# A four-layer graph network on one core: the attention stage of layer 0 with the variance per node by Newton steps, two tiles of layer 1 made early, and loads seven chunks ahead

## The chip, the core and the metric

The kernel runs on one core of a Trainium2 chip. The metric is the device time of one launch in microseconds. Before the change it is the median of three runs, 1951.25 us (1949.47 to 1952.59).

The names in a profile: PE is TensorE (matrix products, into PSUM), PEld its loading of weights, DVE is VectorE, ACT is ScalarE, POOL is GpSimd, SP is SyncE, which here only issues transfers. SPq and POOLq are the queues of transfers that these two issue.

## What is computed

`x` has 8 batches of 2048 nodes with 64 features. There are four layers; each takes `h = max(layernorm(x), 0)` and adds its result to `x`. The change touches the end of layer 0 and the start of layer 1:

```python
# layer 0, end: two candidates per node, mixed by attention scores
def attn_scores(f):
    return jnp.tanh(f @ fcW + fcb) @ av
pair = jnp.stack([industry, g], axis=2)
coefs2 = jax.nn.softmax(attn_scores(pair), axis=-1)
out = jnp.einsum('bnk,bnkf->bnf', coefs2, pair)
x = x + out
# layer 1
h = jnp.maximum(_layernorm(x, axis=-1), 0.0)       # (x - m) / sqrt(v + eps)
h = jnp.matmul(h, W)
s_src, s_dst = jnp.matmul(h, a_src), jnp.matmul(h, a_dst)
e = leaky_relu(s_src[:, :, None] + s_dst[:, None, :], 0.2)
attention = softmax(jnp.where(adj > 0.5, e, NEG_INF), axis=2)
x = x + elu(jnp.matmul(attention, h))
```

A softmax over two candidates is a sigmoid of the difference of their scores, and a sigmoid is a tanh of half the argument. So layer 0's end is: the tanh of each candidate's projection, their difference, the product with `av`, a tanh, and `out = g + (1 + tanh) * (industry - g) / 2`.

## The kernel before

**Layout.** Two batches with 64 features each fill the 128 partitions; this is a pair, and there are four (`p` = 0 to 3). The 2048 nodes lie along the free dimension, in four chunks of 512 (`c`). So the stage at the end of layer 0 works on 16 chunks `(p, c)`, numbered from 0 in the order of pairs. For layer 1 the nodes are also cut into 16 tiles of 128 (`m`).

**The attention stage of layer 0** (the loop at the end of `layer0`, lines 1452 to 1536). `gT[p]`, which the trace calls `hn`, holds `g` of a pair; `industry` lies in DRAM as `ind_dram`. Each chunk goes through these functions:

- `first` loads `iv` from `ind_dram` (line 1475, on SP's queue) and makes `th_s`, the tanh of `fcW` times `iv`: two matmuls into `pf` (PSUM, two buffers for all), one activation of 128x1024 on ScalarE. In the trace a float32 matmul shows as two passes.
- `second` does the same for `g` and then overwrites `iv` with `iv - g/2` on VectorE.
- `differ` subtracts the two tanh tiles (VectorE, 128x1024).
- `third` multiplies by `av` into `pd` (two buffers) and takes the tanh in place.
- `fourth` makes `(tanh + 1) * iv`. For pair 0 it adds `g` and the old `x` (`xo`, loaded by SP, line 1513) on VectorE and SP stores the sum to `x1_dram` (line 1504). For the other pairs POOL issues a transfer that adds the tile to `x1_dram` (line 1500), which the trace calls `xd`; `g` itself is added to it by three transfers of 1 MB from POOL (line 1534, `xd<-hn`).
- After the last chunk of a pair, `late_tile` has POOL load one of the last four tiles of the adjacency, `aTl`, into the memory of that pair's `hn` (line 2188).

The loop runs the functions interleaved: iteration `i` does `first` and `second` of chunk `i + 1`, `third` of `i - 1`, `differ` of `i` and `fourth` of `i - 2`.

**Layer 1's start for pair 0** is woven into this loop. `first_neighbours` is a generator; from iteration 5 the loop takes two of its steps per iteration. For two chunks at a time it makes the mean (a matmul with `avg`, 1/64 in two blocks), subtracts it (`xc`), squares (`q`, ScalarE), makes the variance by a second matmul with `avg` (`var`, which repeats it on all 64 rows of a batch), takes ln and exp on ScalarE for the inverse root, and scales and clips `xc`. Then `ph` is the product with `W1x`: per tile of 128 nodes the 128 features and four scores. `vd`, `wd` and `rs` are exponentials of the scores, and `hS` is the features times `vd`. Last come `R`, a copy of `rs` along the free dimension on every partition (16 matmuls into `pb`, four copies), and `pr`, its transpose, which goes to DRAM for the second half of the nodes. `ph`, `mean`, `var` and `pb` share the two PSUM tags "ln" and "h".

**Layer 1's attention** (`attend`): for each tile `m`, VectorE makes two tiles `pt` of 128x1024, `max(R, wd) * adjacency` (line 1733, one for each batch of the pair; this stands for the leaky relu, the mask and the exponential at once), and TensorE multiplies them with `hS` into `o` and with `vd` into `dn`. Between the tiles, the next pair's norm and maps are woven in by `neighbour_steps`, which reads `x` back from `x1_dram` (line 1575).

**What sets the order.** Instructions go to each engine's own queue and are carried out in that queue's order; a waiting one holds all behind it. A scheduler may reorder what is written, except what goes through `InOrder` (line 631 in the trace: it records the instruction and keeps it in program order) or through `kit.mm` while `kit.strict` is set (line 734). In this stage TensorE, ScalarE (`A`) and VectorE (`V`) are in written order; SP's and POOL's transfers are not. Tile pools hand out memory that may have belonged to an earlier stage, and then the first write waits for the last use there.

## Time and profile before

| what | value |
|---|---|
| median of three runs | 1951.25 us |
| profiled execution: its time, its span | 1953.49 us, 1951.7 us |
| TensorE busy, mean granted clock | 1888.2 us (97%), 0.989 |
| VectorE busy | 1191.2 us (61%) |
| ScalarE busy | 437.4 us (22%) |
| first score matmul of the stage | 374.57 us |
| first `o` matmul of layer 1 | 462.13 us |

How to read it: times are microseconds from the start of the span. A row of the stretches gives, for a stretch of time, its length, then the busy time and the number of instructions of each engine, then the granted TensorE clock as a share of full speed, the busy share of the 16 DMA engines and their rate. A row of the waits gives who waited for whom: the sum, the number of times, the longest. A row in order of time gives start, duration, engine, line, operation, output and inputs, shapes, and in brackets how long the engine was idle before it and what ended that. A wait for several things is put down to the one that came last.

### The profile page before, as it was taken

How to read it: one execution, taken by the hardware profiler on the slowest of the kernel's cores; microseconds unless marked ns; L12 is line 12 of the kernel's file. 1: busy time of each engine (PE TensorE's matmuls, PEld its weight loads, DVE VectorE, ACT ScalarE, POOL GpSimd, SP SyncE). 2: the span in 40 equal slices, each digit the busy share in tenths (PEclk: the TensorE clock that was granted, in tenths of full speed). 3: DMA queues.
4: the chain of work that ended last, by engine and by line, in shares of the span. 5: the costliest groups of instructions: out<-in, count | busy, mean ns of one | idle time of the engine just before them, and what ended most of it. 6: DMA issues, size and time to landing. Idle time of an engine off the chain costs nothing.

```text
span 1951.7 us, 23508 instructions
## 1 busy us (share of the span) xinstructions
PE 1888.2 (97%) x9060; PEld 1141.7 (58%) x9060; DVE 1191.2 (61%) x1917; ACT 437.4 (22%) x923; POOL 310.3 (16%) x435
## 2 busy tenths in 40 slices
PE   7999999888999999999999999999999999999997
PEld 6877767423323232247775567765577755677653
DVE  8676499667899998973327652346723266523465
ACT  6322355564212110111220101301112201012100
POOL 4111187311000000000002110111200022101122
PEclk9999899999999999999999999999999999999999
DMA  7656385374121212214200112101022011121000
GB/s 211 174 177 180 121 249 148 97 200 82 41 62 40 61 43 55 65 23 116 60 22 25 30 43 71 49 10 30 24 74 59 22 25 30 43 71 49 5 19 12
DMA packets 86363, 142.43 MB, mean 73 GB/s; under 512 B 33801, under 2 KB 34057, under 8 KB 83569
## 3 DMA queue, kind: packets, MB, share of 16 engines
q1 hardware_dynamic: 65200, 83.86, 14.8%
q0 software_dynamic: 21040, 56.98, 12.0%
q8 instruction: 73, 1.20, 0.3%
q14 instruction: 50, 0.40, 0.1%
HBM read 106.85 MB, written 37.09 MB: 74 GB/s over the span
## 4 chain that ended last, share of the span: by engine, by line
PE 74%; issue 14%; DVE 4%; DMA 3%; POOL 3%; ACT 1%; SPq 0%; POOLq 0%; DVEq 0%; ACTq 0%
PE acc L734 33%; PE u L734 13%; PE o L734 6%; PE dn L734 3%; PE py L734 3%; PE pgs L734 2%; PE acc L1058 2%; PE pd L734 2%; PE var L734 1%; PE mean L734 1%; DMA iv<-ind_dram 1%; DMA at<-in_adjT 1%; DVE pt L1733 1%; PE pv L734 1%; PE pm L734 1%
## 5 line engine op out<-in xcount | busy, mean ns | idle before, releaser
L734 PE MATMUL acc<-aT,parts 128*128 128x512 f32 x1664 | 462.0, 421 | 0.0
L734 PEld LDWEIGHTS acc<-aT,parts 128*128 128x128 f32 x1664 | 306.6, 188 | 111.8 <-issue 51.3
L734 PE MATMUL u<-W3f,y 64*128 64x512 f32 x1024 | 243.2, 589 | 0.0
L1733 DVE SCALAR_TENSOR_TENSOR pt<-R,wd,aT 128x1024 f32<-128x1024 f32 x192 | 236.1, 1279 | 9.7 <-DMA R<-r_dram 4.7
L734 PE MATMUL o<-pt,hS 128*64 128x512 f32 x1024 | 237.2, 599 | 0.8 <-DVE pt L1733 0.6
L2136 DVE TENSOR_TENSOR pr<-u,embf 128x512 f32<-128x512 f32 x256 | 170.7, 688 | 110.2 <-PE u L734 103.2
L734 PEld LDWEIGHTS u<-W3f,y 64*128 64x128 f32 x1024 | 102.3, 187 | 118.0 <-issue 118.0
L734 PEld LDWEIGHTS o<-pt,hS 128*64 128x64 f32 x1024 | 68.4, 136 | 159.9 <-issue 149.2
L734 PE MATMUL u<-W3f,v 64*128 64x512 f32 x512 | 135.0, 596 | 0.0
L2148 POOL TENSOR_TENSOR fold<-fold 128x256 f32<-128x256 f32 x64 | 47.7, 746 | 498.4 <-DVE fold L2147 498.4
L734 PE MATMUL dn<-pt,vd 128*32 128x512 f32 x1024 | 123.1, 598 | 0.0
L1952 DVE TENSOR_TENSOR yb<-py,cb_f 128x512 f32<-128x512 f32 x32 | 22.1, 691 | 161.3 <-PE py L734 161.3
L1058 PE MATMUL acc<-at,Y 128*128 128x512 f32 x384 | 104.7, 415 | 0.0
L734 PE MATMUL acc<-aTl,parts 128*128 128x512 f32 x384 | 98.8, 395 | 0.0
L2140 DVE TENSOR_TENSOR pr<-pr 128x512 f32<-128x512 f32 x128 | 88.2, 689 | 2.2
L2042 POOL TENSOR_TENSOR bq<-bq,xp 128x512 f32<-128x512 f32 x16 | 20.6, 1289 | 430.1 <-ACT xp L2025 430.1
L1733 DVE SCALAR_TENSOR_TENSOR pt<-R,wd,aTl 128x1024 f32<-128x1024 f32 x64 | 79.8, 1282 | 12.4 <-PE dn L734 8.2
L734 PEld LDWEIGHTS u<-W3f,v 64*128 64x128 f32 x512 | 57.3, 186 | 49.6 <-issue 36.1
L734 PEld LDWEIGHTS acc<-aTl,parts 128*128 128x128 f32 x384 | 71.4, 188 | 16.2
L1058 PEld LDWEIGHTS acc<-at,Y 128*128 128x128 f32 x384 | 70.7, 194 | 14.6 <-issue 1.3
L734 PEld LDWEIGHTS dn<-pt,vd 128*32 128x32 f32 x1024 | 26.9, 108 | 80.9 <-issue 75.9
L1966 DVE TENSOR_TENSOR parts<-tp,parts 128x512 fp32r<-128x512 f32 x16 | 11.1, 692 | 85.7 <-ACT parts L1965 85.7
(354 smaller groups left out, 2688.6 us busy)
## 6 DMA issues: line engine op xcount, KB each, us to landing
at<-in_adjT POOLq DMA_DIRECT2D x32, 512.0 KB, 5.5
raw<-in_adjT SPq DMA_DIRECT2D x64, 256.0 KB, 3.4
aT<-in_adjT POOLq DMA_DIRECT2D x12, 1024.0 KB, 6.2
xp<-xd SPq DMA_DIRECT2D x45, 256.0 KB, 3.0
R<-r_dram SPq DMA_DIRECT2D x14, 512.0 KB, 3.8
hlo<-lo_dram POOLq DMA_DIRECT2D x18, 235.1 KB, 3.7
hhi<-hi_dram POOLq DMA_DIRECT2D x18, 235.1 KB, 3.4
hi_dram<-hi SPq DMA_DIRECT2D x16, 264.0 KB, 3.4
```

Source lines behind the costliest of these rows:

```text
L734: one = self.nc.tensor.matmul(*args, **kw)
L1058: mm(acc[p], Y[h][:, m, p, :], at[:, k, :], start=m + h == 0, stop=m == NT - 1 and h == 1)
L1733: nc.vector.scalar_tensor_tensor(pt, R[b2], wd[:, m, b2 : b2 + 1], aT[m][:, s].bitcast(FP), op0=OP.max, op1=OP.mult)
L1952: nc.vector.tensor_tensor(yb, py, bias[:, None, :].to_broadcast([P, 4, P]), op=OP.add)
L1966: nc.vector.tensor_tensor(lo, tp, hi.bitcast(FP), op=OP.subtract)
L2042: nc.gpsimd.tensor_add(bq, bq, xp)
L2136: nc.vector.tensor_tensor(a, u[h], emb[:, i, 8 * w : 8 * w + 8, None].to_broadcast([P, 8, F]), op=OP.mult)
L2140: nc.vector.tensor_add(pr[h], pr[h], a)
L2148: nc.gpsimd.tensor_add(fold[:, :, 0:2, :], fold[:, :, 0:2, :], fold[:, :, 2:4, :])
```

## The change

The variance moves behind the product with `W1x`. The centred `x` is only clipped at zero, not scaled; since the inverse root is positive, the scale commutes with the clip and the product. For each tile of 128 nodes a further small matmul multiplies the squares with two columns of `avg`, which gives the variance per node and batch, with the nodes on the partitions, beside the features and the scores in `ph`. ScalarE copies the features to `hS`, VectorE copies scores and variance to `raw`. When all 16 tiles are there, VectorE makes the inverse root of 128x32 numbers at once: a first guess by integer operations on the bits and three Newton steps. The scores are scaled by it, and `hS` is scaled by its product with `vd`, a quarter in the stage and three quarters in the first tiles of layer 1's attention. So there is no ln in the stage.

The generator gives way to a `plan`: for each engine and each iteration of the loop, which functions are called. The norm begins in iteration 4 and the last of it stands in iteration 17; `R` is made in iterations 14 and 15, and the `pt` tiles of tiles 0 and 1 (`edge`) in 16 and 17. For this the pool of `pt` is opened before the stage; the tanh tiles come from it too.

The loads of `iv` leave `first` and go to `fetch`: seven before the first matmul, four of them in turn with the loads of `xo`, and then one per iteration for the chunk six after the present one. The pool has eight buffers, not nine. SP's and POOL's transfers of the stage now keep the written order (`S`, `G`), the late adjacency tiles among them, and the three 1 MB adds stand in iterations 3, 7 and 11 rather than 1, 4 and 8.

```diff
-        io = s0.enter_context(tc.tile_pool(name="o_io", bufs=9, reuse_waits="tile"))
+        io = s0.enter_context(tc.tile_pool(name="o_io", bufs=8, reuse_waits="tile"))
...
-            th = sb.tile([P, 2, CW], FP, tag="th", name="th_s", bufs=5)
+            th = one.pt.tile([P, HN], FP, tag="pt", name="th_s").rearrange("p (b n) -> p b n", b=2)
             act.activation(th, pf, AF.Tanh, bias=fcb, scale=f)
             return th
 
+        def fetch(i):
+            p, c = chunks[i]
+            ivs[i] = io.tile([P, CW], FP, tag="iv", name="iv")
+            S.dma_start(out=ivs[i], in_=ind_dram[p, :, cols(c)])
+
         def first(i):
-            p, c = chunks[i]
-            iv = ivs[i] = io.tile([P, CW], FP, tag="iv", name="iv")
-            nc.sync.dma_start(out=iv, in_=ind_dram[p, :, cols(c)])
-            ths[i] = scores(iv, 2.0)
+            ths[i] = scores(ivs[i], 2.0)
...
-                nc.gpsimd.dma_start(out=x1_dram[p, :, cols(c)], in_=df, accum_op=OP.add)
+                G.dma_start(out=x1_dram[p, :, cols(c)], in_=df, accum_op=OP.add)
...
+        G = InOrder(tc, nc.gpsimd)
+        for i in range(3):
+            fetch(i)
+        for c in range(NCW):
+            fetch(3 + c)
+            xs.append(sb.tile([P, CW], FP, tag="x", name="xo", bufs=NCW))
+            S.dma_start(out=xs[c], in_=t["xT"][0, :, cols(c)])
         first(0)
         kit.strict = False
         first(1)
-        for c in range(NCW):
-            xs.append(sb.tile([P, CW], FP, tag="x", name="xo", bufs=NCW))
-            nc.sync.dma_start(out=xs[c], in_=t["xT"][0, :, cols(c)])
         second(0)
-        steps = one.first_neighbours(xs, V, A)
+        near = one.first_neighbours(xs, V, A)
 
         for i in range(len(chunks) + 2):
-            if i > 4:
-                next(steps, None)
+            near("DVE", i)
             if 0 < i < len(chunks) - 1:
                 first(i + 1)
             if i < len(chunks) - 1:
                 second(i + 1)
+            near("PE0", i)
             if 0 < i <= len(chunks):
                 third(i - 1)
+            near("PE", i)
             if i < len(chunks):
                 differ(i)
             if i > 1:
                 fourth(i - 2)
-            if i > 4:
-                next(steps, None)
-            if i in (1, 4, 8):
+            if 0 < i and i + 6 < len(chunks):
+                fetch(i + 6)
+            near("V2", i)
+            near("ACT", i)
+            if i in (3, 7, 11):
                 p = 1 + i // 4
-                nc.gpsimd.dma_start(out=x1_dram[p], in_=gT[p], accum_op=OP.add)
-        for _ in steps:
-            pass
+                G.dma_start(out=x1_dram[p], in_=gT[p], accum_op=OP.add)
...
+        self.lasting = ExitStack()
+        self.pt = self.lasting.enter_context(tc.tile_pool(name="att_pt", bufs=6, side="right", reuse_waits="tile"))
...
+        raw = sb.tile([P, NT, 6], FP, name="raw", bufs=1)
...
-                mm(var[k], kit.avg, q[k], start=True, stop=True)
...
-                A.activation(q[k], var[k], AF.Ln, bias=kit.eps)
-            for k in range(2):
-                A.activation(q[k], q[k], AF.Exp, scale=-0.5)
...
-                V.scalar_tensor_tensor(xc[k], xc[k], 0.0, q[k], op0=OP.max, op1=OP.mult)
...
-                    A.activation(vd[:, ms, :], ph[:, :, P : P + 2], AF.Exp, scale=0.2)
-                for ms, ph in two:
-                    V.tensor_copy(sc[:, ms, :], ph[:, :, P:])
-                    V.tensor_tensor(
-                        hS[:, ms, :].rearrange("p t (b f) -> p t b f", b=2),
-                        ph[:, :, 0:P].rearrange("p t (b f) -> p t b f", b=2),
-                        vd[:, ms, :, None].to_broadcast([P, 2, 2, F]), op=OP.mult,
-                    )
...
+        def centre(c):
+            mean[c] = ps.tile([P, CW], FP, tag=("ln", "h")[c % 2], name="mean")
+            mm(mean[c], kit.avg, xs[c], start=True, stop=True)
+
+        def centred(c):
+            xc[c] = sb.tile([P, CW], FP, tag="xc", name="xc")
+            V.tensor_sub(xc[c], xs[c], mean.pop(c))
+
+        def squared(c):
+            q[c] = sb.tile([P, CW], FP, tag=("x", "q")[c % 2], name="q", bufs=1)
+            A.activation(q[c], xc[c], AF.Square)
+
+        def clipped(c):
+            V.tensor_scalar(xc[c], xc[c], 0.0, None, op0=OP.max)
+
+        def maps(c):
+            for g in range(2):
+                ph = ps.tile([P, 2, P + 6], FP, tag=("ln", "h")[g], name="ph")
+                for j in range(2):
+                    n = slice((2 * g + j) * P, (2 * g + j + 1) * P)
+                    mm(ph[:, j, 0 : P + 4], xc[c][:, n], kit.W1x, start=True, stop=True)
+                    mm(ph[:, j, P + 4 :], q[c][:, n], kit.avg[:, 0:P:F], start=True, stop=True)
+                out.append((NC4 * c + 2 * g, ph))
+
+        def mapped():
+            for m, ph in out:
+                A.activation(hS[:, m : m + 2, :], ph[:, :, 0:P], AF.Copy)
+                V.tensor_copy(raw[:, m : m + 2, :], ph[:, :, P:])
+            out.clear()
+
+        def guess():
+            I32 = mybir.dt.int32
+            V.tensor_scalar(var, raw[:, :, 4:6], EPS, None, op0=OP.add)
+            V.tensor_scalar(rstd.bitcast(I32), var.bitcast(I32), 1, None, op0=OP.logical_shift_right)
+            V.tensor_scalar(rstd.bitcast(I32), rstd.bitcast(I32), -1, 0x5F3759DF, op0=OP.mult, op1=OP.add)
+
+        def newton():
+            V.tensor_tensor(nw, rstd, rstd, op=OP.mult)
+            V.scalar_tensor_tensor(nw, nw, -0.5, var, op0=OP.mult, op1=OP.mult)
+            V.scalar_tensor_tensor(rstd, nw, 1.5, rstd, op0=OP.add, op1=OP.mult)
+
+        def scored():
+            V.tensor_tensor(
+                sc.rearrange("p t (k b) -> p t k b", b=2), raw[:, :, 0:4].rearrange("p t (k b) -> p t k b", b=2),
+                rstd[:, :, None, :].to_broadcast([P, NT, 2, 2]), op=OP.mult,
+            )
+
+        def weights():
+            A.activation(vd, sc[:, :, 0:2], AF.Exp, scale=0.2)
+            A.activation(wd, sc[:, :, 0:2], AF.Exp, scale=0.8)
+            A.activation(rs, sc[:, :, 2:4].rearrange("p t b -> p b t"), AF.Exp, scale=-0.8)
+
+        def weighted():
+            V.tensor_tensor(rstd, rstd, vd, op=OP.mult)
+
+        def scaled(c):
+            h = hS[:, NC4 * c : NC4 * c + NC4, :].rearrange("p t (b f) -> p t b f", b=2)
+            V.tensor_tensor(
+                h, h, rstd[:, NC4 * c : NC4 * c + NC4, :, None].to_broadcast([P, NC4, 2, F]), op=OP.mult
+            )
+
...
+        def spread():
+            for b2, k, pb in out:
+                A.activation(self.first[b2][:, cols(k)], pb.rearrange("p k n -> p (k n)"), AF.Copy)
...
+        plan = {"PE": {}, "DVE": {}, "V2": {}, "PE0": {}, "ACT": {}}
+        for d, i in ((0, 4), (2, 8)):
+            for c in range(d, d + 2):
+                k = i + c - d
+                for e, j, f in (
+                    ("PE", i, centre), ("DVE", i + 1, centred), ("ACT", k + 1, squared), ("DVE", k + 2, clipped), ("PE", k + 2, maps),
+                ):
+                    plan[e].setdefault(j, []).append(at(f, c))
+                plan["DVE"].setdefault(k + 3, []).append(mapped)
+        for e, i, f in (
+            ("V2", 12, guess), ("V2", 12, newton), ("DVE", 13, newton), ("DVE", 13, newton), ("DVE", 13, scored),
+            ("ACT", 13, weights), ("DVE", 14, weighted), ("DVE", 14, at(scaled, 0)),
+            ("PE", 14, at(rows, 0)), ("DVE", 15, spread), ("PE0", 15, at(rows, 1)), ("ACT", 15, spread),
+            ("PE", 16, turn), ("V2", 16, lambda: self.edge(0, V)), ("DVE", 17, stored), ("DVE", 17, lambda: self.edge(1, V)),
+        ):
+            plan[e].setdefault(i, []).append(f)
+        self.scaled = [at(scaled, c) for c in range(1, NCW)]
+
+        def near(engine, i):
+            for f in plan[engine].get(i, ()):
+                f()
+
+        return near
...
+    def edges(self, m, R, wd, a, V):
+
+        pts = []
+        for b2 in range(2):
+            pt = self.pt.tile([P, HN], FP, tag="pt", name="pt")
+            V.scalar_tensor_tensor(pt, R[b2], wd[:, m, b2 : b2 + 1], a.bitcast(FP), op0=OP.max, op1=OP.mult)
+            pts.append(pt)
+        return pts
+
+    def edge(self, m, V):
+
+        self.done[m] = self.edges(m, self.first, self.now[2], self.aT[m][:, cols(0, HN)], V)
...
-            pts = []
-            for b2 in range(2):
-                pt = self.pt.tile([P, HN], FP, tag="pt", name="pt")
-                nc.vector.scalar_tensor_tensor(
-                    pt, R[b2], wd[:, m, b2 : b2 + 1], aT[m][:, s].bitcast(FP), op0=OP.max, op1=OP.mult
-                )
-                pts.append(pt)
+            pts = done.get(m) or self.edges(m, R, wd, aT[m][:, s], nc.vector)
+            if m and self.scaled:
+                self.scaled.pop(0)()
...
+        def load(m, a, queue=nc.gpsimd):
+            queue.dma_start(out=a, in_=kit.adj_rows(m, slice(0, N)))
...
-            load(NT - NP + p, low.tile([P, N], FR, tag=f"hn{p}", name=f"aTl{p}"))
+            load(NT - NP + p, low.tile([P, N], FR, tag=f"hn{p}", name=f"aTl{p}"), InOrder(tc, nc.gpsimd))
```

## The prediction

> **What bounds the kernel now.** I read the page first, then the busy time by stretches, then who TensorE waited for in the stage that the change touches, then that stage in order of time.
>
> ```profile
> PE 1888.2 (97%) x9060; PEld 1141.7 (58%) x9060; DVE 1191.2 (61%) x1917; ACT 437.4 (22%) x923; POOL 310.3 (16%) x435
> ```
>
> TensorE is the bound of the whole, so only its unbusy or slow time can be won. The stage from the first score matmul (374.57 us) to layer 1's first `o` matmul (462.13 us) holds much of it:
>
> ```profile
> core 0: us, PE busy (x) PEld busy (x) DVE busy (x) ACT busy (x) POOL busy (x), PEclk, DMA share, GB/s
> 374.57:462.13 87.56, 69.42 (x275) 26.32 (x274) 54.51 (x81) 59.07 (x83) 15.31 (x19) 0.92 0.78 186
> ```
> ```profile
> 389.74:400.19 10.45, 9.50 (x29) 3.09 (x29) 7.42 (x10) 5.32 (x6) 0.00 (x0) 0.84 1.02 265
> ...
> 411.53:422.00 10.47, 6.31 (x20) 2.46 (x21) 4.47 (x9) 8.55 (x12) 1.74 (x2) 0.67 0.75 197
> ```
>
> TensorE idles 87.56 - 69.42 = 18.1 us here, and behind two of its gaps the granted clock falls to 0.84 and 0.67. The waits in this stretch:
>
> ```profile
> PE pf L734 <- DMA iv<-ind_dram: 5.6, 3, 2.6
> PE pf L734 <- ACT th_s L631: 4.2, 1, 4.2
> PE ph L734 <- DVE xc L631: 3.2, 1, 3.2
> PE var L734 <- ACT q L631: 1.9, 2, 1.4
> PE ph L734 <- DVE hS L631: 1.4, 1, 1.4
> ```
>
> 5.6 us wait for loads of `iv`. Most of the rest belongs to the norm and maps of layer 1. In order of time:
>
> ```profile
> 375.10 4.58 SPq L1475 DMA_DIRECT2D iv<-ind_dram  x7
> 375.64 2.80 POOL L1534 DMA_DIRECT2D xd<-hn  x3 [6.65 <-ACT hn L631]
> ...
> 389.74 2.08 PE L734 MATMUL pf<-iv,fcWf 64*128 64x512 f32 x4 [2.64 <-DMA iv<-ind_dram]
> ...
> 409.62 1.28 ACT L631 ACT_TABLE_LOAD   x1
> 410.91 1.27 ACT L631 ACTIVATE q<-var,eps_f 128x512 f32<-128x512 f32 x2
> 412.19 1.28 ACT L631 ACT_TABLE_LOAD   x1
> 413.49 1.15 ACT L631 ACTIVATE q<-q 128x512 f32<-128x512 f32 x2
> 414.54 2.10 ACT L631 ACTIVATE th_s<-pf,fcbf 128x1024 f32<-128x1024 f32 x2
> 415.69 2.08 PE L734 MATMUL pf<-iv,fcWf 64*128 64x512 f32 x4 [4.16 <-ACT th_s L631]
> ```
>
> The seven loads share the DMA engines with three 1 MB adds that POOL issues in one go. ScalarE then works 4.9 us on ln and exp with a table load before each (409.62 to 414.54), while the tanh that frees a score buffer stands behind them. Where nothing interferes, a chunk takes 2.93 us (score matmuls start at 437.20 and again at 440.13).
>
> **The present stage in a sum.** At full clock: 16 chunks x 2.93 = 46.9; two `mean` and two `var` pairs at 1.91 (435.29 to 437.20) = 7.6; four `ph` groups at 1.10 (420.90 to 422.00) = 4.4; the 32 `pb` passes and `pr` 4.1. That is 63.0. Busy is 69.4, so 6.4 us are half-clock loss; with 18.1 idle the sum is 87.5.
>
> **Part 1: no ln, variance per node.** Removed: the two `var` pairs (3.8 us of TensorE), four table loads (4 x 1.28), two pairs of ln (1.27 us) and two of exp (1.15), four 0.69 us scale-and-clip operations. Added: 16 `avg` matmuls with two columns. Nearest rows: one pass of `pm` with 16 columns every 0.11 us, one pass of `ph` with 132 every 0.137 us; two passes each make 3.5 to 4.4, and I take 3.8, nearer `pm`. TensorE's work stays at 63.0 - 3.8 + 3.8 = 63. ScalarE gets eight copies of 128x256 (between 0.36 for 128x114 and 0.60 for 128x512, say 0.42, 3.4 us in all), spread two to a chunk beside 2.65 us of tanh per chunk: 3.4 us in such a chunk, while TensorE needs 2.93 + 1.10 + 0.95 = 5.0 there, so they are hidden. Clips are plain scalar operations from SBUF, 0.42 us (row of `t<-agg`).
>
> Here the Trainium skill and the row differ: "ScalarE: Activation LUTs", What ACT_TABLE_LOAD costs, charges a drain of about 1.38 us beside the 1.28 us load, 2.66 per switch. Four switches would give 10.6 us back by the page; in the rows the next activation starts 1.29 us after the load starts, so 5.1. I use the row, and of it only what stood on TensorE's path.
>
> **Newton.** Guess 3 operations, three steps of 3, one scaling: 13 dependent VectorE operations, plus one that multiplies in `vd`. Nearest: 128x8 scalar operations at 0.19 us; dependent ones start 0.03 after the end, so 0.22 each, 2.9 us (if they overlapped, 0.1 each, 1.3; at 0.26, 3.4). They lie in iterations 12 and 13, where VectorE then has about 8 us and TensorE 5.9; about 1 us of slack precedes, so 1.2 us reach TensorE through `differ`, which the `pd` matmul needs.
>
> **Part 2: loads ahead, adds spread.** Of the adds, `hn` 1 still starts near 375.6 (first on POOL, its wait is on ScalarE's copy); 2 and 3 go behind the fourth steps of chunks 5 and 9. The eleven loads of SP are issued before any of these two, so the 5.6 us of load waits and their half clock go. POOL now keeps the written order, so a late adjacency tile that waits for the last score matmul of a pair holds the adds behind it; that tile's buffer is read for the last time before those adds are due. Two prices. First, in the built order chunk 1's load waits for the last `gn` of the stage before (373.91 us), through reused memory; before it was there early. With the least landing of 2.8 us TensorE waits 376.8 - 375.53 = 1.3 us, with the median 5.9 us 4.4. All other loads of SP stand behind it. Until chunk 2's score, TensorE has 3.84 us of work and now takes 6.47; then the two score buffers still wait for tanh at 1.06 each. I take 3.5 us lost (1.9 to 5.5). Second, with eight buffers the loads of chunks 12 to 15 wait for the adds of chunks 4 to 7; those of 6 and 7 stand behind the 1 MB add of `hn` 2. On SP the load of `x` for the next pair and the store of `rr` stand behind them. I count zero, because each is issued three to five chunks before its use; this is the open term (second rival).
>
> Here a rule speaks against the change. "TensorE: Matmul & The Clock Gate", What's actually happening: the clock halves after an idle window of about 3.4 us. By that length the new wait for chunk 1 costs itself alone. In the trace a gap of 2.64 us was enough (score matmuls of 2.08 for 1.13), one of 1.99 at 381.04 was not. By the row, a wait past 2.6 us costs another 1.8 us; my 3.5 takes part of it.
>
> **VectorE for pair 0.** Its chunks cost 0.61 + 1.14 + 3 x 0.72 = 3.9 us, four of them in a row against 2.93, now with two centrings (1.3) where TensorE has only one `mean` pair: 16.9 against 13.6. I charge 2.5 us after slack.
>
> **Part 3: tiles 0 and 1 inside the stage.** Four `pt` operations at 1.28 (1.22 apart) and `R` move before the last `pd` matmuls are done. At the end TensorE still waits for the second pair's `R` copies and the first `pt`: 2.3 us (now 457.33 to 462.13 holds 0.7, and 0.8 ahead of `pb`). The tanh tiles come from the six buffers of `pt` (five of their own before); the first `pt` takes one freed two chunks earlier, no cost. Three of the four `hS` scalings (0.61 each, 1.8 us) go into layer 1, where VectorE is near its limit:
>
> ```profile
> 640.00:660.00 20.00, 20.00 (x123) 5.53 (x124) 18.66 (x16) 0.00 (x0) 0.00 (x0) 1.00 0.10 32
> ```
>
> They stand ahead of the next pair's centring, which `var` and `ph` of TensorE wait for: 1.0 us paid back (0 to 2.1). The last step of chunk 15, its add and the last adjacency load come behind the `pt`s; that tile is used 14 tiles x 2.8 us later, so it is covered.
>
> **Sum.** New stage: 63 of work + 3.5 + 2.5 + 1.2 + 2.3 = 72.5, against 87.5: 15.0 won, 1.0 paid back, 14.0. The profiled execution took 1953.49 us (span 1951.7), so 1939.5; it lies 2.2 above the median of 1951.25, from which 1937.2 follows.
>
> **Rivals.** (a) As summed, 1937.2; own range 1934 to 1941; 0.62. (b) Waits overlap better than I charge: start 1.9, pair 0 1.0, Newton 0, end 1.5, paid back 0: 67.4 against 87.5, 20.1 won, 1931; for it, VectorE is busy only 54.5 of 87.6 us; 0.13. (c) The load ring binds: DMA is at 1.02 busy in 389.74 to 400.19, and an add landed after 17.1 us (median of `hn`). Behind such a `hn` 2, issued near 410, add 6 lands at 433 and load 14 at 436, some 5 us after its use near 431, and the half clock takes 2 more: 14 - 7 = 7 won, 1944; against it, only one large add is in flight then; 0.18. (d) The same place, worse: if the add of `hn` 2 takes past 25 us, every later load of SP slides by 13 us and more, and with 18 us late at half clock 2 us, 14 - 20 = 6 lost: 1957; it decides from about 14 us of lateness; 0.04. (e) VectorE in layer 1 gives everything back, no change: its tiles need 2.44 us against TensorE's 2.79, so the backlog drains; 0.03.
>
> **How the numbers follow.** 0.2% (3.9 us) is about what a measurement here can tell from no change. Faster: a, b, and c nearly whole, 0.93; same: e, 0.03; slower: d, 0.04. The range of 8 in 10 reaches over the centres of b and c: 1931 to 1945.
>
> **What would show it.** No table load between 375 and the end of the stage; no `iv` wait except chunk 1's; first `o` matmul 13 to 16 us earlier, near 447; granted clock 1.0 from 385 to 445. Wrong would be: waits of `pf` on `iv` at chunks 12 to 15, a half-clock stretch in the first 10 us, or the `o` of tile 5 no more than 8 us earlier.

## The result, and the profile after

The changed kernel takes 1937.6 us (median of 6 runs, 1934.66 to 1941.83); the kernel before, with three further runs, 1953.59 us. The ratio is 0.9914 with a 95% interval of 0.9895 to 0.9933: 13 to 21 us less. The profiled execution took 1935.01 us with a span of 1933.2 us, against 1953.49 and 1951.7 us before: 18.5 us less. The forecast was 1937.2 us, reckoned from the first three runs of the kernel before (1951.25 us).

The stretch from the first score matmul to the first `o` matmul of layer 1, in the table by stretches (length, busy time of TensorE, its weight loads, VectorE, ScalarE, GpSimd, then granted clock, DMA share, rate):

```profile
core 0: us, PE busy (x) PEld busy (x) DVE busy (x) ACT busy (x) POOL busy (x), PEclk, DMA share, GB/s
373.93:442.78 68.85, 62.98 (x298) 26.80 (x297) 52.96 (x88) 51.15 (x72) 14.03 (x17) 1.00 0.89 217
```

87.56 us became 68.85. The clock is full all the way, so no time is lost at half clock, and 5.87 us of idle time are left of 18.1. The waits of TensorE in it (sum, times, longest) are these:

```profile
PE pd L734 <- DVE iv L631: 1.6, 2, 1.0
PE pf L734 <- DMA iv<-ind_dram: 1.5, 1, 1.5
PE pr L741 <- ACT R L631: 0.8, 1, 0.8
PE ph L734 <- DVE xc L631: 0.7, 1, 0.7
PE o L734 <- DVE pt L631: 0.6, 1, 0.6
PE pf L734 <- ACT th_s L1469: 0.3, 1, 0.3
PE pf L734 <- ACT th_s L631: 0.3, 1, 0.3
```

One load is still waited for, chunk 1's. Before, loads took 5.6 us and the tanh behind ln and exp 4.2 us in one piece. So far this is the picture that the prediction drew.

The rest of the kernel was expected to change by 1 us. It changed by more, in two places that nearly cancel. The first is at the end of layer 1, where the last pair of batches begins. SP's queue, VectorE and TensorE after, in order of time:

```profile
724.23 24.15 SPq L1752 DMA_DIRECT2D R<-r_dram  x2
```
```profile
752.52 6.07 DVE L1765 SCALAR_TENSOR_TENSOR pt<-R,wd,aT 128x1024 f32<-128x1024 f32 x5 [4.48 <-DMA R<-r_dram]
```
```profile
753.86 3.67 PE L734 MATMUL o<-pt,hS 128*64 128x512 f32 x6 [4.70 <-DVE pt L1765]
757.47 2.91 PE L734 MATMUL dn<-pt,vd 128*32 128x512 f32 x16
```

and SP's queue before, at the same point:

```profile
742.64 0.81 SPq L1696 DMA_DIRECT2D R<-r_dram  x2
```

The two loads of `R` for the last pair were issued within 0.81 us of each other; now the second stands 24 us behind the first. SP's queue waits there for an `o` matmul of TensorE:

```profile
SPq L1752 <- PE o L734: 23.5, 1, 23.5
```

VectorE waits 4.5 us for the load, TensorE 4.7, and the matmuls behind that gap run at half clock at first (16 `dn` matmuls in 2.91 us, elsewhere in 1.92).

The second place is all of the later layers. They use tiles `parts`, made in the pool of `pt`. Their two groups of matmuls (minimum, median and maximum of one, in ns), before and after:

```profile
L734 PE MATMUL acc<-aT,parts x1664: 388/396/800, 869.2 to 1914.5; 128*128 128x512 f32 x185
...
L734 PE MATMUL acc<-aTl,parts x384: 387/393/478, 875.2 to 1916.3; 128*128 128x512 f32 x192
```
```profile
L734 PE MATMUL acc<-aT,parts x1664: 387/389/799, 857.3 to 1896.5; 128*128 128x512 f32 x185
L734 PE MATMUL acc<-aTl,parts x384: 392/397/479, 863.1 to 1898.3; 128*128 128x512 f32 x192
```

The 1664 matmuls with `aT` got 7 ns shorter, the 384 with `aTl` 4 ns longer, though nothing of these instructions was changed. Where two of the first kind follow each other, the second starts 227 ns after the first in the median instead of 233; summed over all such places this is 6.7 us, and the other kind gives 0.7 us back. One layer's step of 269.7 us takes 268.2.

The two profiled executions, stretch by stretch, from marks that both have:

| stretch | before | after | difference |
|---|---|---|---|
| start of span to first score matmul | 374.57 | 373.93 | -0.64 |
| first score matmul to first `o` | 87.56 | 68.85 | -18.71 |
| first `o` to the last pair's `pr` | 278.49 | 279.42 | +0.93 |
| that `pr` to the first `mean` of layer 2 | 40.55 | 47.13 | +6.58 |
| that `mean` to the end of the span | 1170.53 | 1163.87 | -6.66 |
| sum | 1951.70 | 1933.20 | -18.50 |

### The profile page after: what moved, and what is told of

The parts are those of the page before. It is cut to its first block, busy times and chain, and to the rows that moved or that the text cites. A ratio compares the mean times of both kernels' runs of the same rounds, so it can differ in the third digit from the quotient of the medians.

```text
span 1933.2 us, 23540 instructions
## 1 busy us (share of the span) xinstructions
PE 1875.9 (97%) x9084; PEld 1140.7 (59%) x9084; DVE 1192.1 (62%) x1927; ACT 429.5 (22%) x912; POOL 311.6 (16%) x435
## 4 chain that ended last, share of the span: by engine, by line
PE 70%; issue 17%; DVE 5%; DMA 4%; POOL 2%; ACT 1%; POOLq 0%; SPq 0%; DVEq 0%; ACTq 0%
PE acc L734 32%; PE u L734 13%; PE o L734 4%; PE py L734 3%; PE pd L734 2%; PE acc L1058 2%; PE pgs L734 2%; PE dn L734 2%; DMA at<-in_adjT 1%; DMA den<-d_dram 1%; PE pf L734 1%; PE mean L734 1%; DVE pt L1765 1%; PE var L734 1%; PE ph L734 1%
## 5 line engine op out<-in xcount | busy, mean ns | idle before, releaser
L734 PE MATMUL acc<-aT,parts 128*128 128x512 f32 x1664 | 454.7, 417 | 0.0
L1765 DVE SCALAR_TENSOR_TENSOR pt<-R,wd,aT 128x1024 f32<-128x1024 f32 x188 | 231.6, 1277 | 14.1 <-DMA R<-r_dram 8.2
```

The lines of the kernel that those rows point to most:

```text
L734: one = self.nc.tensor.matmul(*args, **kw)
L1765: V.scalar_tensor_tensor(pt, R[b2], wd[:, m, b2 : b2 + 1], a.bitcast(FP), op0=OP.max, op1=OP.mult)
```

## The experiments

The work before the first score matmul ends between 371.3 and 380.0 us in the profiled executions, though the code there is the same in all kernels. So the traces are compared from that matmul on, and the launches by their ratio to runs of the kernel before that were taken beside them (1950.5 to 1953.9 us in the median); the medians of two rows are not always from the same chip. "Stage" is the second row of the table above.

| kernel | launch, median us | ratio to before (95%) | stage | `pr` to `mean` | `mean` to end | first score to end |
|---|---|---|---|---|---|---|
| before | 1953.59 | 1 | 87.56 | 40.55 | 1170.53 | 1577.13 |
| changed | 1937.6 | 0.9914 (0.9895 to 0.9933) | 68.85 | 47.13 | 1163.87 | 1559.27 |
| e1_loads_alone | 1953.53 | 1.0021 (1.001 to 1.0032) | 87.18 | 40.35 | 1169.73 | 1576.34 |
| e2_adds_alone | 1948.04 | 0.999 (0.9978 to 1.0002) | 83.66 | 40.40 | 1170.04 | 1571.26 |
| e3_norm_alone | 1953.24 | 1.0005 (0.9989 to 1.002) | 83.69 | 46.35 | 1164.68 | 1574.60 |
| e4_no_tiles | 1935.61 | 0.9919 (0.9899 to 0.9938) | 67.98 | 46.91 | 1164.25 | 1556.84 |
| e5_loads_and_pool | 1940.77 | 0.9952 (0.9935 to 0.9969) | 82.35 | 40.68 | 1164.61 | 1565.20 |
| e6_norm_and_adds | 1945.58 | 0.997 (0.9958 to 0.9982) | 77.66 | 46.08 | 1163.92 | 1567.07 |
| e7_adds_at_once | 1944.14 | 0.9959 (0.9944 to 0.9974) | 78.24 | 47.10 | 1164.45 | 1568.65 |
| e8_start_free | 1932.9 | 0.991 (0.989 to 0.9929) | 67.30 | 47.32 | 1164.62 | 1558.26 |
| e9_root_by_ln | 1942.31 | 0.9934 (0.9908 to 0.996) | 69.97 | 46.55 | 1164.57 | 1561.06 |
| e10_newton_six | 1937.77 | 0.9916 (0.989 to 0.9941) | 70.96 | 46.18 | 1164.35 | 1561.03 |
| e11_hs_later | 1930.07 | 0.9873 (0.9847 to 0.99) | 68.77 | 40.74 | 1164.44 | 1553.79 |
| e12_three_fixed | 1925.63 | 0.9855 (0.9827 to 0.9883) | 66.61 | 40.82 | 1164.12 | 1549.78 |

A single profiled execution differs from what the ratios say by 2 to 5 us in several rows; of the launch the ratio counts, the trace tells where the time lies.

### Does the gain add up from its parts?

The prediction added the parts. That is theory A: one hole made by late loads, another by ln and exp, independent of each other. The rival B is that the norm is all of the gain and hides the loads.

**e1_loads_alone.** The kernel before with part 2 alone.

```diff
+        G = InOrder(tc, nc.gpsimd)
+        for i in range(3):
+            fetch(i)
+        for c in range(NCW):
+            fetch(3 + c)
...
-            if i in (1, 4, 8):
+            if 0 < i and i + 6 < len(chunks):
+                fetch(i + 6)
+            if i in (3, 7, 11):
```

> The kernel before with part 2 alone: loads ahead in written order, eight buffers, the three 1 MB adds in iterations 3, 7 and 11; norm with ln as before. Theory A (two holes that add up): the load waits of 5.6 us and 1.8 us of half clock go, the wait of chunk 1's load for gn brings about 1.5 us back, so the stage from the first score matmul to the first o takes 87.6 - 5.9 = about 81.7 us (80 to 83), the launch about 6 us less; the half-clock stretch at the ln pair stays. Rival B (the loads were hidden behind the norm's waits, the norm alone is the gain): stage 86 to 88, no gain over 2 us.

The stage took 87.18 us and the launch 0.2% more than before. By the number, rival B is right, but not by its reason. The trace has the gain of A first: chunk 9's score starts 407.37 - 371.26 = 36.1 us after the first, before 415.69 - 374.57 = 41.1. It is lost at the end of the stage. (That the launches are 2 to 6 us longer than before isn't in this trace, which is 0.8 us shorter from the first score matmul on.) VectorE, then TensorE there:

```profile
457.09 1.29 DVE L1741 SCALAR_TENSOR_TENSOR pt<-R,wd,aT 128x1024 f32<-128x1024 f32 x1 [6.99 <-DMA xd<-iv]
```
```profile
458.44 4.96 PE L734 MATMUL o<-pt,hS 128*64 128x512 f32 x8 [4.62 <-DVE pt L1741]
```

The first `pt` waits 7 us for a transfer `xd<-iv`. In this kernel the pool of `pt` is opened behind the stage, and its first tile falls on the memory of `iv` tiles that are still being added to `x1_dram`. TensorE waits 4.6 us and then runs eight matmuls in 4.96 us that take 3.13 in the changed kernel. The changed kernel opens that pool before the stage; a side of part 3 that the prediction had down as "no cost" was what let part 2 keep its gain.

**e2_adds_alone.** Only the adds are spread; SP's loads and the nine buffers stay as before.

```diff
-                nc.gpsimd.dma_start(out=x1_dram[p, :, cols(c)], in_=df, accum_op=OP.add)
+                G.dma_start(out=x1_dram[p, :, cols(c)], in_=df, accum_op=OP.add)
...
-            if i in (1, 4, 8):
+            if i in (3, 7, 11):
```

> The kernel before with one thing of part 2: POOL's transfers in written order and the 1 MB adds in iterations 3, 7 and 11; SP's loads stay as they were. Theory A, with the crowd of three adds as the cause of the late loads: iv waits fall from 5.6 us to under 2 and the stage takes 80 to 82.5 us, as with the whole of part 2 or 1 us less, since chunk 1's load doesn't wait for gn. Rival C (it is the order and depth of SP's loads that matters): iv waits stay over 4 us and the stage over 85 us.

The loads behave nearly as A expects: one wait of 2.04 us is left of 5.6, where under 2 was expected. The stage is 83.66, 1.2 us over the expected range. Half clock after that one wait is part of it: 2.08 and 1.79 us for two groups that take 1.13 and 1.02. On the launch the gain can't be told from none.

**e3_norm_alone.** The changed kernel with the old loads and adds.

```diff
-            S.dma_start(out=ivs[i], in_=ind_dram[p, :, cols(c)])
+            nc.sync.dma_start(out=iv, in_=ind_dram[p, :, cols(c)])
...
-            if i in (3, 7, 11):
+            if i in (1, 4, 8):
```

> The changed kernel with the loads and adds of the kernel before (eight buffers): parts 1 and 3 alone. Theory A: the load waits of 5.6 us with their half clock come back, stage 68.9 + 5.9 = about 74.8 us (73 to 77), the launch 10 to 12 us under the kernel before. Rival B: stage 69 to 70.5, as good as the whole change. Rival D (the holes hide each other, so that each alone gains little): stage over 80 us.

Theory A falls: the norm alone won 3.9 us of stage and nothing on the launch. Rival D has the number right. The reason is one wait that the kernel before does not have. TensorE, then the issues of GpSimd and of SP's queue:

```profile
397.32 2.08 PE L734 MATMUL pf<-iv,fcWf 64*128 64x512 f32 x4 [12.97 <-DMA iv<-ind_dram]
```
```profile
379.38 2.80 POOL L1535 DMA_DIRECT2D xd<-hn  x3 [5.13 <-ACT hn L631]
```
```profile
380.07 4.23 SPq L1475 DMA_DIRECT2D iv<-ind_dram  x6
```

and in the kernel before:

```profile
375.10 4.58 SPq L1475 DMA_DIRECT2D iv<-ind_dram  x7
...
375.64 2.80 POOL L1534 DMA_DIRECT2D xd<-hn  x3 [6.65 <-ACT hn L631]
```

Before, the loads began 0.5 us ahead of the first of the three adds. Here they begin 0.7 us behind it, and chunk 2's comes 13 us late. It is the loads that moved: the adds begin 1.1 us after the first score matmul in both kernels. With eight buffers chunk 1's load must wait for the last `gn`, and the others of SP stand behind it:

```profile
SPq L1475 <- DVE gn L631: 21.1, 1, 21.1
```

Eight buffers are what fits once the pool of `pt` is open during the stage; in the built program no byte is free between the stage's pools and that of the norm. So the parts are not independent: the pool takes a buffer, the lost buffer makes the loads late, and then the adds decide how late.

**e4_no_tiles.** Part 3 without its early tiles.

```diff
-            ("PE", 16, turn), ("V2", 16, lambda: self.edge(0, V)), ("DVE", 17, stored), ("DVE", 17, lambda: self.edge(1, V)),
+            ("PE", 16, turn), ("DVE", 17, stored),
```

> The changed kernel without part 3's early tiles: the pt tiles of tiles 0 and 1 are made in layer 1's attention, as before. Theory A: the last step of chunk 15 and the store of rr come ahead of the first pt on VectorE, about 1 us; the first o comes 0.5 to 1.5 us later and nothing else changes, so stage 69.4 to 70.4. Rival E (the early tiles are most of what was won at the end): 2.5 to 5 us later, since VectorE is behind from tile 1 on.

Both theories had the sign wrong: the first `o` comes 0.9 us earlier than in the changed kernel, the end of the span 2.4 us (1556.84 against 1559.27). The launch can't tell the two apart. Left to the scheduler, the first `pt` falls into time in which VectorE waited for a tanh: it starts 442.79 - 377.86 = 64.93 us after the first score matmul, in the changed kernel 441.45 - 373.93 = 67.52. The waits of `ph` on `hS` in the first tiles of layer 1 (1.8 us after) are gone too.

### What do the loads need?

Theory F: the crowd of adds delays the loads, and the pool of `pt` decides whether the end keeps what was won. Its rivals: G, the end waits anyway; H, the order and depth of SP's loads decide, not the adds.

**e5_loads_and_pool.** e1_loads_alone with the pool opened ahead of the stage.

```diff
+        self.pt = self.lasting.enter_context(tc.tile_pool(name="att_pt", bufs=6, side="right", reuse_waits="tile"))
         self.near = near = ExitStack()
...
-            th = sb.tile([P, 2, CW], FP, tag="th", name="th_s", bufs=5)
+            th = one.pt.tile([P, HN], FP, tag="pt", name="th_s").rearrange("p (b n) -> p b n", b=2)
```

> The kernel before with part 2 and the pool of pt opened before the stage, with the tanh tiles in it; norm with ln, no early tiles. Theory F (part 2 alone won 5 us by chunk 9 and lost it at the end, where the first pt was written into memory of iv tiles whose transfers were still under way: 4.6 us of wait and 1.8 us of half clock): both go, stage 87.2 - 6.4 = 80.8 us (79.5 to 82), the launch about 6 us under the kernel before. Rival G (the end waits for those transfers in any case, or for something as late): stage over 85 us, no gain.

The wait at the end is gone and the stage falls from 87.18 to 82.35, 0.4 us over the expected range: F, not G. The launch gained 0.5%, more than the stage explains. From the `mean` of layer 2 to the end it takes 1164.61 us against 1169.73 in e1. The matmuls there are the shorter ones:

```profile
L734 PE MATMUL acc<-aT,parts x1664: 387/389/803, 862.1 to 1901.5; 128*128 128x512 f32 x185
```

e1 and e5 differ only in that pool and in the tanh tiles that come from it. In the built programs the adjacency tiles lie at the same addresses in both; `parts` does not. All ten other kernels with the pool ahead of the stage have 1163.9 to 1164.7 in that column, those without 1169.7 to 1170.5. So where the pool lies is worth 5 to 7 us in layers that the change doesn't name.

**e6_norm_and_adds.** e3_norm_alone with the adds spread and in order; SP's loads as before.

```diff
-            if i in (1, 4, 8):
+            if i in (3, 7, 11):
```

> Parts 1 and 3 and of part 2 only POOL's written order with the 1 MB adds in iterations 3, 7 and 11; SP's loads as in the kernel before, with eight buffers. Theory F (three adds in one go put the loads 13 us late, the order of SP's loads matters little): iv waits fall from 14.4 to 2 to 4 us, stage 69 to 72 us, the launch within 3 us of the changed kernel. Rival H (loads that are issued behind those of xo and the first add come late anyway): iv waits over 6 us, stage over 75.

**e7_adds_at_once.** The changed kernel with the three adds in one go; loads ahead and in order.

```diff
-            if i in (3, 7, 11):
-                p = 1 + i // 4
+            if i in (1, 2, 3):
+                p = i
```

> The changed kernel with its loads in written order, but the 1 MB adds in iterations 1, 2 and 3. Theory F (it is the crowd of adds that delays loads): iv waits of 8 to 13 us at chunks 2 to 5 with a half-clock stretch behind them, stage 78 to 84 us, launch 9 to 15 us slower than the changed kernel. Rival H (order and depth of the loads decide): iv waits under 4 us, stage under 72.

TensorE's longest wait in e6, with GpSimd's add and SP's loads there, and then the longest wait in e7:

```profile
386.68 2.08 PE L734 MATMUL pf<-iv,fcWf 64*128 64x512 f32 x4 [7.56 <-DMA iv<-ind_dram]
```
```profile
374.01 0.94 POOL L631 DMA_DIRECT2D xd<-hn  x1 [3.68 <-ACT hn L631]
```
```profile
374.70 5.07 SPq L1475 DMA_DIRECT2D iv<-ind_dram  x6
```
```profile
397.97 2.08 PE L734 MATMUL pf<-iv,fcWf 64*128 64x512 f32 x4 [6.39 <-DMA iv<-ind_dram]
```

F is right for e7 (whose launch is some 9 us over the changed kernel's by the ratios, the low end of what F said) and wrong for e6, where H is right. With both halves of part 2 the load waits are 1.5 us and the stage 68.85; with the loads ahead and in order alone 9.7 and 78.24; with the spread alone 9.2 and 77.66; with neither 14.4 and 83.69. In e6, SP issues the four loads of `xo` first, so those of `iv` go out 0.7 us behind a single 1 MB add, which is enough for 7.6 us. The loads of `xo` alone are not the reason: they stand ahead in e2 too, and there chunk 2's load, issued 0.5 us ahead of the add, lands after 5.9 us; in e6 it lands after 11.8 us, 0.2 us behind the add. In e7 the loads of chunks 2 and 3 are ahead of the adds and come in time; those of chunks 4 and 5 are not.

### The prices

**e8_start_free.** Two pools of the stage are opened in the other order, so that another load lies in the memory that the last `gn` reads.

```diff
-        io = s0.enter_context(tc.tile_pool(name="o_io", bufs=8, reuse_waits="tile"))
         sb = s0.enter_context(tc.tile_pool(name="o_sb", bufs=2, reuse_waits="tile"))
+        io = s0.enter_context(tc.tile_pool(name="o_io", bufs=8, reuse_waits="tile"))
```

> The changed kernel with the pools of the loads and of the small tiles opened in the other order, so that another load than chunk 1's lies in the memory of gn (chunk 5's). Theory A: the 1.5 us wait of the second score matmul goes, chunk 2's score starts 4.3 to 4.8 us after the first instead of 5.95, and the stage takes 67.0 to 67.8 us. Rival I (pair 0 is bound by VectorE, which gives the 1.5 us back by chunk 5): stage 68.4 to 69.2.

The first two score matmul pairs run as one group:

```profile
380.04 1.99 PE L734 MATMUL pf<-iv,fcWf 64*128 64x512 f32 x8
```

Chunk 2's score starts 4.75 us after it (5.95 in the changed kernel), and the stage is 67.30: theory A. The wait for chunk 1 cost what it showed.

**e9_root_by_ln.** Newton's steps against ln and exp on the same 128x32 numbers.

```diff
+        def root():
+            A.activation(var, raw[:, :, 4:6], AF.Ln, bias=kit.eps)
+            A.activation(rstd, var, AF.Exp, scale=-0.5)
...
-            ("V2", 12, guess), ("V2", 12, newton), ("DVE", 13, newton), ("DVE", 13, newton), ("DVE", 13, scored),
+            ("ACT", 12, root), ("DVE", 13, scored),
```

> The changed kernel with the inverse root of the same 128x32 numbers made by ln and exp on ScalarE in iteration 12 instead of the 12 Newton operations on VectorE; variance per node as in the changed kernel. Two table loads of 1.28 us and two small activations hold ScalarE 3.0 us; a chunk needs 2.65 us of ScalarE against 2.93 of TensorE, so most of it reaches TensorE, and the 1.0 us wait for Newton goes. Theory A (price of the ln by the rows of before): first score to first o 69.3 to 71 us against 68.85. Rival K (a switch costs 2.66 us, by the Trainium skill, ScalarE: Activation LUTs, What ACT_TABLE_LOAD costs, so 5.8 us and a half clock behind it): 72.5 to 75 us. Rival L (in this place ScalarE has room, Newton's steps were not needed): 68 to 69 us.

The stage is 69.97, 1.1 us more than with Newton: theory A. ScalarE in order of time:

```profile
427.82 1.28 ACT L631 ACT_TABLE_LOAD   x1
429.11 0.32 ACT L631 ACTIVATE varn<-raw,eps_f 128x32 f32<-128x32 f32 x1
429.45 1.28 ACT L631 ACT_TABLE_LOAD   x1
430.75 0.23 ACT L631 ACTIVATE rstd<-varn 128x32 f32<-128x32 f32 x1
430.88 2.10 ACT L631 ACTIVATE th_s<-pf,fcbf 128x1024 f32<-128x1024 f32 x2
```

The activations start 1.29 and 1.30 us after their loads start, and from the first load to the next tanh it is 3.06 us. The 2.66 us per switch of rival K, the price of the Trainium skill ("ScalarE: Activation LUTs", What ACT_TABLE_LOAD costs), are not seen here. TensorE waits 2.1 us for the tanh and is spared the 1.0 us for Newton. So of the ln, only 1.1 us is left to win once the variance is per node; the kernel before held ScalarE for 4.9 us with ln and exp of 128x512 tiles, and that twice.

**e10_newton_six.** Three more Newton steps, nine operations.

```diff
-            ("DVE", 13, newton), ("DVE", 13, newton),
+            ("DVE", 13, newton), ("DVE", 13, newton), ("DVE", 13, newton), ("DVE", 13, newton), ("DVE", 13, newton),
```

> The changed kernel with six Newton steps instead of three: nine more dependent VectorE operations of 128x32 in iteration 13, at 0.22 us 2.0 us. Theory A (the chain is exposed; its 1.0 us wait is what it costs already): the wait of pd on VectorE grows from 1.0 to 3.0 us, stage 70.7 to 71.2 us, or 1 us more where the gap halves the clock behind it. Rival M (VectorE has slack there and the wait is of another cause): stage under 69.6 us.

```profile
434.82 1.08 PE L734 MATMUL pd<-th_s,Avf 128*64 128x512 f32 x4 [3.03 <-DVE iv L631]
```

The wait grew from 0.98 to 3.03 us, the stage from 68.85 to 70.96: each further operation reaches TensorE in full, 2.1 us for nine, 0.23 each.

### The loss at the last pair

In the built program, the second load of `R` waits for the last `o` matmul of pair 2, which reads `hS`: the pool for the late `R` is opened where the pool of the norm was, and in the changed kernel `hS` is laid out first in that pool, ahead of the tiles `q` and `xc`, so the new `R` falls on it. Theory P says that this is the loss, rival Q that the transfer is slow for another reason.

**e11_hs_later.** The tiles `q` and `xc` are made first, then `hS`.

```diff
-        hS = sb.tile([P, NT, P], FP, tag="hS", name="hS", bufs=1)
-        mean, xc, q, out = {}, {}, {}, []
+        mean, out = {}, []
+        q = {c: sb.tile([P, CW], FP, tag=("x", "q")[c], name="q", bufs=1) for c in range(2)}
+        xc = {c: sb.tile([P, CW], FP, tag="xc", name="xc") for c in range(2)}
+        hS = sb.tile([P, NT, P], FP, tag="hS", name="hS", bufs=1)
```

> The changed kernel with hS laid out behind the tiles of the norm in its pool, as in the kernel before, so that the late R tile of the last pair doesn't lie in the memory of pair 2's hS; nothing else. Theory P (that overlap makes SP's second load of R for the last pair wait 24 us for the last o matmul of pair 2, from which TensorE loses 4.7 us and 2 us of half clock): the stretch from the last pr to the mean of layer 2 falls from 47.1 to 40.5 us, stage unchanged at 68.9, the launch 6 to 7 us faster than the changed kernel. Rival Q (R comes late for another reason, a crowd of transfers at that time): the stretch stays at 46 to 47 us.

```profile
729.25 0.80 SPq L1756 DMA_DIRECT2D R<-r_dram  x2
```

Both loads go out in 0.80 us, the stretch is 40.74 us instead of 47.13, and no other stretch moved by more than 0.6 us: theory P. The launch is at 0.9873 of the kernel before.

**e12_three_fixed.** The edits of e11_hs_later, e8_start_free and e4_no_tiles together; of each the line that tells most:

```diff
-        mean, xc, q, out = {}, {}, {}, []
+        q = {c: sb.tile([P, CW], FP, tag=("x", "q")[c], name="q", bufs=1) for c in range(2)}
...
-        io = s0.enter_context(tc.tile_pool(name="o_io", bufs=8, reuse_waits="tile"))
         sb = s0.enter_context(tc.tile_pool(name="o_sb", bufs=2, reuse_waits="tile"))
+        io = s0.enter_context(tc.tile_pool(name="o_io", bufs=8, reuse_waits="tile"))
...
-            ("PE", 16, turn), ("V2", 16, lambda: self.edge(0, V)), ("DVE", 17, stored), ("DVE", 17, lambda: self.edge(1, V)),
+            ("PE", 16, turn), ("DVE", 17, stored),
```

> The changed kernel with three things: hS laid out as in e11_hs_later, the two pools exchanged as in e8_start_free, no early tiles as in e4_no_tiles. Theory A (the three lie in different places and add up): 6.6 us at the last pair, 1.5 at the start, 1.9 in the first tiles of layer 1, from the first score matmul to the end of the span 1559.3 - 10.0 = 1549.3 us (1548 to 1551), about 28 us under the kernel before, ratio 0.986. Rival R (one is paid for elsewhere): over 1552.

From the first score matmul to the end 1549.78 us, expected 1548 to 1551; launch 1925.63 us, 0.9855 (0.9827 to 0.9883) of the kernel before. This version is better than both.

## Why the prediction was right, and where it was not

The time, 1937.6 us, is the forecast of 1937.2 but for 0.4 us, and that closeness is in part luck. The forecast gain was 14.0 us; the medians of six runs each give 16.0, the ratio 13 to 21, the two profiled executions 18.5. The kernel before took 2.3 us more in its six runs than in the three that the forecast started from. By its own steps the prediction is right in part, and in part errors cancel.

**The stage.** 72.5 us were predicted, 68.85 measured. TensorE's work at full clock was put at 63.0 and is 62.98; half clock was put at zero and is zero. All four charges for waits were too high:

| term | predicted | measured |
|---|---|---|
| start, chunk 1's load | 3.5 | 2.10 (1.48, 0.35, 0.27) |
| VectorE for pair 0 | 2.5 | 1.33 (0.62, 0.71) |
| Newton | 1.2 | 0.98 |
| end | 2.3 | 1.46 (0.82, 0.64) |
| sum | 9.5 | 5.87 |

The mechanisms were the right ones, each shown by its row and two of them by an experiment (e8, e10). The sizes of the start and of pair 0 were taken between bounds that were wide, and both ended near the lower one. The 3.6 us by which they were too high are won beyond the forecast. For the whole stage rival (b), that the waits overlap better (67.4 us), was nearer than the likeliest case.

**Stat matmuls.** 3.8 us were charged. A group of maps takes 403.25 - 401.37 = 1.88 us against 1.10, so four cost 3.1. That the sum of TensorE's work came out all the same is luck: the other terms together were 0.7 us too low.

**Newton.** Thirteen operations at 0.22 us were put at 2.9 us. The first and the last of them on VectorE in the changed kernel:

```profile
428.97 0.17 DVE L631 TENSOR_SCALAR varn<-raw 128x32 f32<-128x32 f32 x1
...
431.66 0.23 DVE L631 TENSOR_TENSOR sc<-raw,rstd 128x64 f32<-128x64 f32 x1
```

From 428.97 to 431.89 it is 2.9 us.

**Paid back in layer 1.** Charged 1.0 us. TensorE waits 1.8 us for `hS` in the first tiles, and 0.9 us is left of it at the last `pr`. The size was right, the reason only half: e4 has the same three scalings of `hS` in these tiles, and without the early `pt` tiles nothing waits for `hS` there and the stretch takes 277.71 us, 0.8 less than before. So the price is that of the scalings and the early tiles together. What failed is the sum, which has nothing else outside the stage: nothing was said of where the tiles lie afterwards. The new order of tiles in the norm's pool cost 6.6 us at the last pair (e11 gives 6.4 of it back), the new place of the pool of `pt` won 6.7 us in the later layers (e5 shows 5.1 of it against e1). Neither was in the ledger, and their sum is -0.1. Had the last pair's `R` not been hit, the forecast would have been over 6 us too high.

**The parts as a sum.** That the load waits "go" was right for the change as a whole and wrong as a property of one edit. The spread of the adds alone, or the order of the loads alone, leaves 9 us of waits beside the new norm; part 2 without the moved pool loses all at the end; the norm without part 2 wins nothing on the launch. With part 2 and the pool in place (e5), the new norm takes the stage from 82.35 to 68.85 us. Of these 13.5 us Newton's steps are 1.1 (e9), and the early tiles cost 0.9 (e4). Whether the rest comes from the variance per node or from the new order of the functions was not tried. The prediction had the link between eight buffers and `gn` and priced it at the start only, because the adds were spread at the same time.

**The rivals.** (c) and (d), the load ring: SP did wait 19.9 us in all for the adds of earlier chunks, but the last load was issued near 423 and no wait of `pf` on `iv` followed at chunks 12 to 15. The add of `hn` 2 that (c) put at 17.1 us landed after 10.7. (e), all given back in layer 1: not so; but 6.6 us were, at the last pair and for another reason.

**The table load.** The prediction used the row (1.29 us) and not the page's 2.66. e9 confirms the row with its own pair of loads.

**What it said would show.** No table load before the end of the stage, no `iv` wait but chunk 1's, full clock: all there. The first `o` came 19.4 us earlier by the clock of the trace (0.64 of it before the stage), where 13 to 16 were named.

## What to carry to other kernels

Price a moved or resized pool by what its new memory touches: for each tile laid out there, ask what last used that memory and what stands in the queue behind the wait; here this decided 4.6 us (e1), 6.4 (e11) and 13 (e3), more than any instruction that was added. An ablation of one part is not its worth when parts share buffers and queues: test the halves together as well as alone. And read the whole trace against the old one in stretches between common marks, even when the total is as forecast.

## What the hardware showed that was not expected

- **Place of the weights.** Matmuls `acc<-aT,parts` take 389 or 390 ns in the median where the pool of `parts` is opened ahead of the stage and 396 elsewhere; `acc<-aTl,parts` 397 and 393. The instructions are the same. e1 and e5 show that the pool's place does it: with the adjacency tiles where they were, `parts` moved from 54,656 to 106,464 bytes into a partition. Why is open.
- **Half clock and the length of a gap.** The prediction took 2.64 us as enough and 1.99 as too short. In e2 a gap of 2.04 us was followed by half clock (`pf` in 2.08 us instead of 1.13), in e9 one of 2.09 was not (1.13), and in e10 one of 3.03 was not (`pd` in 1.08 us, as ever). The last two come after more than 10 us without a gap, the first after gaps of 1.79, 0.88 and 0.36 us in the 12 us before it. The length of the single gap doesn't decide; the 3.4 us of the Trainium skill ("TensorE: Matmul & The Clock Gate", What's actually happening) fit e9 and e10, and neither e2 nor the 2.64 us of the kernel before. Half clock can also come late: in the kernel before, a gap of 3.16 us (at 446.28) was followed by a `ph` group of 1.17 us at full clock, and only the score matmuls behind it slowed (1.77 and 1.92). What does decide wasn't tried.
- **Order of issue against a 1 MB add.** Begun half a microsecond ahead of three adds, the loads cost 5.6 us of waits (before); 0.7 us behind the first of three, 13.0 (e3); 0.7 us behind a single one, 7.6 (e6). Chunk 1's own wait for `gn`, 1.5 and 1.6 us, is left out.
